# A graph attention layer on one core: the rows of every 32nd pair gathered as x in the node phase, and x_r computed in the rounds of edges

## The chip, the core and the metric

The kernel runs on one core of a Trainium2 chip. The core has a matrix engine (PE), three engines for elementwise work (VectorE or DVE, ScalarE or ACT, GpSimd or POOL), a sync engine (SP) that mostly issues DMAs, and 16 DMA engines. Each engine has a queue of its own and works through it in order; between engines there are semaphores only. The metric is the time on the device, in microseconds.

## The reference

12,500 nodes with 128 features, 400,000 edges sorted by their destination, 32 features an edge, 8 heads of 16.

```
h  = relu(layernorm(x))                       # 12500 x 128
ln = layernorm(h) * g1 + b1
x_l, x_r = ln @ W_l, ln @ W_r
m  = leaky_relu(x_l[src] + x_r[dst] + edge_attr @ W_e, 0.2)    # per edge; each node also has an edge to itself
alpha = per head: sum over 16 of m * att
a  = softmax of alpha over the edges of one destination
h2 = h + sum over edges of a * x_l[src] + bias
out = x + h2 + gelu(layernorm2(h2) @ W1 + b1) @ W2 + b2
```

What matters here: each edge needs the row `x_l[src]`, and `src` is random; `x_r[dst]` is needed in the order of the edges, since `dst` is sorted.

## The kernel before

Nodes are padded to 98 tiles of 128. The **node phase** (`tile_gnn`, lines 211 to 552) takes the tiles in 25 groups of four, `qs`, in a software pipeline: in round `r` the stages of `node_stages` (lines 514 to 527) work on group `r - late`. Statistics of x (`x_stats`, L421 to L423), relu of the normalised x in place in `h_sb` (L433), transposes (`h_turn`, L444), sums of squares (L458), the product with `[W_r | W_l]`, 256 columns (`product`, L468), scaling and bias on DVE (`x_lr`, L477). The result's x_l half, with eight columns of ones behind it (136 columns in all), goes to `xl_dram` (L485); the x_r half is split on POOL into three bf16 parts that add up to it (`split`, L492 to L496) and goes to `xs_dram`. The gain and the bias of the first norm are folded into the weights (`weights`). Between the rounds stand `from_first` (round 6: destinations as bf16 offsets from the first one of each unit; a cast on DVE, L336, and a subtraction on POOL, L340), `fits` (round 8: does the fast path apply?) and `edge_constants` (round 10). SP's queue has, in this order: x's first 16 tiles, the loads of `dst` (`load_dst`: `dc`, 111 rows of 14 KB, and `lu`, the last destination of each unit), the rest of x, constants (`load_consts`, with `att_c`, `we_sb` and `src_sb`), and then the stores of the phase.

The **rounds of edges** (`window_edges`) take 512 edges at a time, a *pair* of units of 256; there are 782 pairs. Everything is recorded by hand in order (`tc.manual_schedule`): in round `r` each entry `(late, f)` of `stages` does `f(r - late)`. For a pair `c`:

- `gather` in round c - 4: four indirect DMAs on POOL (L700), each 128 rows of 136 floats of `xl_dram`, by the column of `src_sb`. The buffers, `rows`, are a ring of twelve;
- `windows` in round c - 3, on SP: `ea` and `dlw` (the edges' features and destinations, for four pairs at a time, pool `load`) and `xrw`, the x_r parts of the 32 nodes the pair can touch;
- `place` (DVE, L728), one round ahead: which edge belongs to which node;
- `combine` in round c (PE): z = transposed rows (L742) + x_r of the destination (L745) + edge features (L746), one PSUM bank;
- `slope` (ACT, L752) and `bend` (DVE, L757) in c + 1: leaky relu; `score` (PE, L763, L764) in c + 2; `lowest` (DVE, L771) and `weigh` (ACT, exponential, L782) in c + 3; `turn` (PE, L790) in c + 4; `keep_turned` (ACT, L795) in c + 5; `collect` (PE, L804) in c + 6; `own_heads` (DVE, L813, L819) in c + 7; `put` (SP) in c + 8 writes the partial sums to `state`.

PSUM has eight banks: two each for `z`, `ab`, `pt_ps`, `acc`. Beside this, in the first 196 rounds the sum over all edge features is taken (`sum_load`, `sum_up`), and from round 199 on the 25 groups of nodes are finished by `steps` (`f_load` to `f_store`, 20 rounds a group, a new group every 23 rounds until they have caught up and every 32 then): the sums are put together, the feed-forward part is done and `out` is written. Their functions of ACT (root, gelu) need other tables than the exponential, which are loaded by ACT_TABLE_LOAD.

Of the kernel before, what the change touches and what calls it, by code (L numbers as in the profile page):

```python
# [46 lines left out]
SPARE = 8  # L47
BIG = 2.0**126
# [60 lines left out]
def heads_of(nc, pool, out, att_c):  # L109

    fh = pool.tile([P, H, C], F32, name="fh")
    iota(nc, fh, [[-1, H], [-H, C]], 0, 1)
    nc.vector.tensor_scalar(fh, fh, 0.0, None, op0=OP.is_equal)
    of = pool.tile([P, H], F32, name="of")
    nc.vector.tensor_reduce(of, fh, AX.X, OP.max)
    nc.vector.tensor_scalar(out, of, att_c, None, op0=OP.mult)
# [3 lines left out]
def tile_gnn(  # L120
# [46 lines left out]
    du_dram = dram.tile([RP * RU * U], BF16, name="du_dram")  # L167
    state = [dram.tile([NT * P * H, SH], F32, name=f"state{i}") for i in range(2)]
# [5 lines left out]
    flag = keep.tile([1, 1], I32, name="flag")  # L174

# [23 lines left out]
    lr_ps = pre.enter_context(tc.tile_pool(name="lr_ps", bufs=2, space=PSUM))  # L199
# [9 lines left out]
    quads = [(t, min(GN, NT - t)) for t in range(0, NT, GN)]  # L209
# [7 lines left out]
    def load_consts():  # L217
        for i, v in enumerate((ln2_g, ln2_b, None, b1[0:P], b1[P : 2 * P])):
            if v is not None:
                nc.sync.dma_start(cols[:, 2 + i : 3 + i], column(v))  # L220
        nc.sync.dma_start(att_c, bass.AP(tensor=att.tensor, offset=att.offset, ap=[[1, C], [C, H], [1, 1]]))
        nc.sync.dma_start(we_sb, bass.AP(tensor=w_e.tensor, offset=w_e.offset, ap=[[P, DE], [0, QP], [1, P]]))
        nc.sync.dma_start(w1_sb, w1)
        nc.sync.dma_start(w2_sb, w2.rearrange("(k p) f -> p k f", p=P))
        nc.sync.dma_start(bias_r, row_bcast(bias, P))
        nc.sync.dma_start(b2_r, row_bcast(b2, P))
        nc.sync.dma_start(src_sb, src)
        nc.sync.dma_start(first_sb, bass.AP(tensor=dst.tensor, offset=dst.offset, ap=[[0, 1], [U, NU]]))

# [40 lines left out]
    wlr = build.tile([P, 2, C, H], F32, name="wlr")  # L270
    bw_r = build.tile([P, 2, C, H], F32, name="bw_r")

    def weights():
        mean = build.tile([P, P], F32, name="mean")
        nc.vector.memset(mean, 1.0 / P)
        b_b = build.tile([P, P], F32, name="b_b")
        nc.scalar.copy(b_b, b1n_c.to_broadcast([P, P]))
        for i, w in enumerate((wr_sb, wl_sb)):
            nc.vector.tensor_scalar(wlr[:, i], w.rearrange("p (h c) -> p c h", c=C), g1_c, None, op0=OP.mult)
        wlr_f = wlr.rearrange("p s c h -> p (s c h)")  # L280
        ps = once_ps.tile([P, 2 * P], F32, name="w_ps")
        nc.tensor.matmul(ps, mean, wlr_f, start=True, stop=True)
        nc.vector.tensor_sub(wlr_f, wlr_f, ps)
        ps = once_ps.tile([P, 2 * P], F32, name="w_ps")
        for i, w in enumerate((wr_sb, wl_sb)):
            nc.tensor.matmul(ps[:, i * P : (i + 1) * P], b_b, w, start=True, stop=True)
        nc.vector.tensor_copy(bw_r, ps.rearrange("p (s h c) -> p s c h", s=2, h=H))

    def edge_constants():
# [4 lines left out]
        heads_of(nc, build, attbd, att_c)  # L294
# [3 lines left out]
        nh = build.tile([P, H, NW], F32, name="nh")  # L298
        iota(nc, nh, [[-1, H], [-H, NW]], 0, 1)
# [4 lines left out]
        own = build.tile([P, NW, H], F32, name="own")  # L304
        iota(nc, own, [[-1, NW], [0, H]], -NC3, 1)
        nc.vector.tensor_scalar(own, own, 0.0, None, op0=OP.is_equal)
        last = build.tile([P, NW, H], F32, name="last")
        iota(nc, last, [[0, NW], [0, H]], -NC3 - NW, 1)
# [3 lines left out]
        third = build.tile([P, CW], F32, name="third")  # L312
        iota(nc, third, [[-NS, CW]], 0, 1)
        group_range(nc, build, third, NS, CW)
        node = build.tile([P, CW], F32, name="node")
        iota(nc, node, [[1, CW]])
        nc.vector.tensor_mul(third, third, node)
        nc.vector.tensor_reduce(nid, third, AX.X, OP.add)
        unit = build.tile([P, 1], F32, name="unit")
        iota(nc, unit, [[0, 1]], -NC3, 1)  # L320
        nc.vector.tensor_scalar(unit, unit, 0.0, None, op0=OP.max)
        nc.vector.tensor_add(nid, nid, unit)
        fq = build.tile([P, QP, DE], F32, name="fq")
        iota(nc, fq, [[-1, QP], [-QP, DE]], 0, 1)
# [23 lines left out]
    def fits():  # L348
# [27 lines left out]
        place = rng.tile([RP, RU], F32, name="place")  # L376
        iota(nc, place, [[1, RU]], 0, RU)
# [17 lines left out]
    qs = [{"t0": t, "n": n, "h": h_sb[:, t : t + n, :]} for t, n in quads]  # L395

# [6 lines left out]
    def root_of(d, r, k):  # L403
        if r not in roots:
            roots[r] = (node.tile([P, 2, GN], F32, name="n_r", bufs=6), [0, 0])
        t, ns = roots[r]
        ns[k] = d["n"]
        d[f"r{k}"] = t[:, k, 0 : d["n"]]
        return d[f"r{k}"]

    def slots(r):
        if r not in roots:
            return []
        t, ns = roots[r]
        return [t] if ns == [GN, GN] else [t[:, k, 0:n] for k, n in enumerate(ns) if n]
# [14 lines left out]
    def relu(d, r):  # L430
        col(d, "sum")
        for t in range(d["n"]):
            nc.scalar.activation(  # L433
                d["h"][:, t, :], d["h"][:, t, :], AF.Relu,
                bias=d["m1"][:, t : t + 1], scale=d["r0"][:, t : t + 1], accum_out=d["sum"][:, t : t + 1],
            )

    def h_mean(d, r):
        nc.vector.tensor_scalar(d["sum"], d["sum"], -1.0 / P, None, op0=OP.mult)
# [14 lines left out]
    def h_square(d, r):  # L454
        col(d, "ssq")
        for t in range(d["n"]):
            sq = node.tile([P, P], F32, name="sq")
            nc.scalar.activation(  # L458
                sq, d["h"][:, t, :], AF.Square, bias=d["sum"][:, t : t + 1], accum_out=d["ssq"][:, t : t + 1]
# [4 lines left out]

    def product(d, r):
        d["lr"] = lr_ps.tile([P, GN, 2 * P], F32, name="lr")
        for t in range(d["n"]):
            nc.tensor.matmul(  # L468
                d["lr"][:, t, :], d["hT"][:, t, :], wlr.rearrange("p s c h -> p (s c h)"), start=True, stop=True
            )  # L470

    def x_lr(d, r):
        n = d["n"]
        d["xlr"] = node.tile([P, GN, P + XW], F32, name="xlr")
        nc.gpsimd.memset(d["xlr"][:, :, 2 * P :], 1.0)
        for t in range(n):
            nc.vector.scalar_tensor_tensor(  # L477
                d["xlr"][:, t, 0 : 2 * P],
                d["lr"][:, t, :],
                d["r1"][:, t : t + 1],  # L480
                bw_r.rearrange("p s c h -> p (s c h)"),
# [3 lines left out]
        nc.sync.dma_start(xl_t[:, d["t0"] : d["t0"] + n, :], d["xlr"][:, 0:n, P:])  # L485

    def split(d, r):
        n = d["n"]
        xr = d["xlr"][:, 0:n, 0:P]
        parts = node.tile([P, GN, NS, P], BF16, name="parts")[:, 0:n]  # L490
        left = node.tile([P, GN, P], F32, name="left")[:, 0:n]
        nc.gpsimd.tensor_copy(parts[:, :, 0, :], xr)  # L492
        nc.gpsimd.tensor_sub(left, xr, parts[:, :, 0, :])
        nc.gpsimd.tensor_copy(parts[:, :, 1, :], left)
        nc.gpsimd.tensor_sub(left, left, parts[:, :, 1, :])
        nc.gpsimd.tensor_copy(parts[:, :, 2, :], left)  # L496
        nc.sync.dma_start(xs_t[:, d["t0"] : d["t0"] + n, :, :], parts)
# [4 lines left out]
    def clear(g):  # L502
# [12 lines left out]
        (8, x_lr),  # L515
# [5 lines left out]
        (9, split),  # L521
    )
    LAST = 9
    with tc.manual_schedule():
        make_identity(nc, ident)
        load_weights()
        load_x(0, min(GN, NT))
        load_x(GN, min(3 * GN, NT - GN))
        load_dst()
        for t in range(4 * GN, NT, 14):  # L530
            load_x(t, min(14, NT - t))
        load_consts()
        nc.gpsimd.memset(empty, 0.0)
        nc.gpsimd.memset(empty[:, :, C + 1 : SH], CAP)
        for r in range(max(len(qs), 2) + LAST + 1):
            if r == 3:
                weights()
            if r == 6:
                from_first()
            if r == 8:  # L540
                fits()
            if r == 10:
                edge_constants()
# [4 lines left out]
            for late, f in node_stages:  # L548
                if 0 <= r - late < len(qs):
                    f(qs[r - late], r)  # L550
        clear(0)
# [3 lines left out]
    with tc.If(fast == 1) as cmp:  # L555
        window_edges(
            tc, n_edges, ea_t, NT, NE, NUE, ident, ident_b, wer, we_z, negrep, diag, nid, farw, bias_r, b2_r, w1_sb, w2_sb,
            cols, xl_dram, xl_t, xs_dram, xs_t, dc_dram, du_dram, state, clear, x_t, out_t, h_sb, src_sb, first_sb,
        )
    with cmp.Else():  # L560
        any_edges(
            tc, n_edges, dst, dst_tiles, ea_t, NT, NG, NCH, CPP, CP, ident, w_e, att, att_c, bias_r,
            xl_dram, xl_t, xs_t, h_sb, src_sb,
# [70 lines left out]
def window_edges(  # L634
    tc, n_edges, ea_t, NT, NE, NUE, ident, ident_b, wer, we_z, negrep, diag, nid, farw, bias_r, b2_r, w1_sb, w2_sb,
    cols, xl_dram, xl_t, xs_dram, xs_t, dc_dram, du_dram, state, clear, x_t, out_t, h_sb, src_sb, first_sb,
# [11 lines left out]
    AHEAD = 4  # L648
    WAHEAD = 3
# [6 lines left out]
    pairs = [{} for _ in range(n_pr)]  # L656

# [8 lines left out]
    with ExitStack() as es:  # L666
        once = es.enter_context(tc.tile_pool(name="e_once", bufs=1))
        load = es.enter_context(tc.tile_pool(name="e_load", bufs=3))
# [27 lines left out]
        def gather(c):  # L696
            xs = rows.tile([P, KP, XW], F32, name="xs")
            for t in tiles_of(c):
# [50 lines left out]
        def slope(c):  # L749
            d, e = pairs[c], sum(edges_of(c))  # L750
            d["zs"] = work.tile([P, EPR], F32, name="zs")
# [293 lines left out]
        def f_store(d):  # L1045
# [10 lines left out]
            (LATE + 1, own_heads),  # L1056
            (0, combine),
# [7 lines left out]
            (5, keep_turned),  # L1065
# [42 lines left out]
        def in_round(r, table):  # L1108
            for k, f in table:
                for d in groups:  # L1110
                    if d["round"] + k == r:
                        f(d)

        CLEAR = 8
        with tc.manual_schedule():
            for r in range(-AHEAD, max(last_round, groups[-1]["round"] + 20)):
# [11 lines left out]
                in_round(r, steps)  # L1128
                for late, f in late_stages:
# [5 lines left out]
def any_edges(  # L1135
    tc, n_edges, dst, dst_tiles, ea_t, NT, NG, NCH, CPP, CP, ident, w_e, att, att_c, bias_r,
    xl_dram, xl_t, xs_t, h_sb, src_sb,
# [31 lines left out]
    with tc.tile_pool(name="build", bufs=1) as build:  # L1169
        nc.vector.memset(attbd, 0.0)  # L1170
        for i in (0, LO):
            heads_of(nc, build, attbd[:, i : i + H], att_c)
# [6 lines left out]
        nc.vector.scalar_tensor_tensor(pick, kh, float(LO), high, op0=OP.is_equal, op1=OP.add)  # L1179

# [302 lines left out]
```

## Time and profile before

| | us |
|---|---|
| runs shown: median of 3 (lowest to highest) | 4172.99 (4167.11 to 4175.78) |
| the profiled execution: its time | 4170.51 |
| its span in the profile | 4168.6 |
| busy: PE / weight loads of PE | 3562.9 / 2472.1 |
| busy: DVE / ACT / POOL | 2433.0 / 1802.9 / 3073.7 |
| mean granted clock of PE | 0.946 |

A group in the profile is written "line engine operation output<-input"; a line of a timeline has the start and the length in us, the engine, the line and the operation, a count, and in brackets the idle time before it and what ended it. `PEld` is PE loading weights, `SPq` and `POOLq` are the queues in which DMAs are issued. "issue" names a wait that nothing in the profile explains. A line of the list of waits has the total, the count and the longest. PEclk is the granted clock of PE as a share of the full one.

### The profile page before, as it was taken

To read this page: it belongs to the slowest core of one execution; us is meant where nothing else is said; L and a number is where in the kernel's file an instruction comes from. 1 tells how busy PE (TensorE), PEld (TensorE's weight loads), DVE (VectorE), ACT (ScalarE), POOL (GpSimd) and SP (SyncE) were. 2 spreads that over 40 slices of the span, in tenths; PEclk is the share of its full clock that TensorE was granted. 3 is DMA by queue.
4 is the path that set the end of the run, shared out by engine and by line. 5 is a ranking of instruction groups with operands and counts; after the bars stand their busy time and mean duration, and the time that the engine had idled before them with its cause. 6 is when DMAs were issued, how large, how long until landed. Compare 5 with 4: busy or idle time off the path is not lost. (4 is left out here: it accounts for less than half of the span.)

```text
span 4168.6 us, 65325 instructions
## 1 busy us (share of the span) xinstructions
PE 3562.9 (85%) x18674; PEld 2472.1 (59%) x18675; DVE 2433.0 (58%) x5279; ACT 1802.9 (43%) x3939; POOL 3073.7 (74%) x3303
## 2 busy tenths in 40 slices
PE   2488888888888898989899989889889999988985
PEld 2355555655566666666666666566666666665654
DVE  6655656656665555655555555565556564655554
ACT  4533333333334444444444444444444444434433
POOL 3977777777777777777777777777777777777772
PEclk8799999999999999999999999999999999999998
DMA  5577777666656555555655566555566565555562
GB/s 150 172 169 182 182 180 179 156 153 159 150 118 116 115 116 119 115 112 115 125 117 117 117 119 120 117 117 105 117 122 118 117 120 113 107 117 104 114 123 51
DMA packets 631298, 535.20 MB, mean 128 GB/s; under 512 B 381763, under 2 KB 520882, under 8 KB 630690
## 3 DMA queue, kind: packets, MB, share of 16 engines
q1 hardware_dynamic: 530354, 313.00, 30.8%
q0 software_dynamic: 100000, 217.80, 29.6%
q8 instruction: 153, 2.51, 0.3%
q14 instruction: 215, 1.76, 0.2%
q10 hardware_dynamic: 576, 0.13, 0.0%
HBM read 477.18 MB, written 53.34 MB: 127 GB/s over the span
## 5 line engine op out<-in xcount | busy, mean ns | idle before, releaser
L700 POOL DMA_INDIRECT xs<-xl_dram,src_sb x3125 | 2955.1, 946 | 952.5 <-issue 808.9
L782 ACT ACTIVATE p<-ab,rec 128x256 f32<-128x256 f32 x1563 | 655.2, 470 | 1678.4 <-DVE rec L771 1654.1
L813 DVE TENSOR_TENSOR own<-acc,diag 128x272 f32<-128x272 f32 x782 | 344.7, 441 | 1360.3 <-PE acc L804 1353.6
L742 PE MATMUL z<-ident,xs 128*128 128x128 f32 x3125 | 585.7, 286 | 474.2 <-DMA xs<-xl_dram,src_sb 467.6
L742 PEld LDWEIGHTS z<-ident,xs 128*128 128x128 f32 x3125 | 405.0, 142 | 945.0 <-DMA xs<-xl_dram,src_sb 563.5
L804 PE MATMUL acc<-xs,pt 128*128 128x136 f32 x6250 | 884.6, 286 | 0.2 <-DVE f_yo L1051 0.2
L746 PE MATMUL z<-ea,we_z 128*128 128x512 f32 x1564 | 859.1, 633 | 0.0
L804 PEld LDWEIGHTS acc<-xs,pt 128*128 128x128 f32 x6250 | 812.5, 197 | 0.4 <-PE pt_ps L790 0.4
L764 PE MATMUL ab<-m,negrep 128*128 128x512 f32 x1564 | 801.1, 594 | 0.0
L752 ACT ACTIVATE zs<-z 128x512 f32<-128x512 f32 x782 | 474.7, 607 | 494.7 <-PE z L746 453.8
L790 PEld LDWEIGHTS pt_ps<-ident,p 128*128 128x128 f32 x3125 | 417.9, 149 | 453.6 <-issue 424.2
L771 DVE TENSOR_REDUCE rec<-ab 128x2 f32<-128x512 f32 x781 | 540.6, 692 | 135.9 <-PE ab L764 128.5
L757 DVE TENSOR_TENSOR m<-z,zs 128x512 f32<-128x512 f32 x782 | 532.2, 681 | 54.2 <-ACT zs L752 54.1
L790 PE MATMUL pt_ps<-ident,p 128*128 128x128 f32 x3125 | 498.2, 285 | 1.7 <-ACT pt L795 1.7
L795 ACT COPY pt<-pt_ps 128x512 f32<-128x512 f32 x782 | 457.6, 585 | 0.0
L819 DVE TENSOR_REDUCE rec<-own 128x34 f32<-128x272 f32 x782 | 341.0, 436 | 26.6
L746 PEld LDWEIGHTS z<-ea,we_z 128*128 128x128 f32 x1564 | 314.6, 201 | 35.7
L764 PEld LDWEIGHTS ab<-m,negrep 128*128 128x128 f32 x1564 | 301.8, 193 | 37.4 <-issue 0.7
L745 PE MATMUL z<-ne,xrw 128*128 128x512 bf16 x782 | 311.3, 398 | 0.0
L728 DVE TENSOR_SCALAR ne<-dlw,nid 112x512 bf16<-112x512 bf16 x782 | 288.5, 369 | 25.6 <-DMA dlw<-du_dram 25.6
L763 PE MATMUL ab<-ne,farw 128*128 128x512 bf16 x782 | 300.9, 385 | 0.0
L839 DVE TENSOR_REDUCE part<-ea_s 128x1 f32<-128x1024 f32 x98 | 118.5, 1209 | 0.0
(165 smaller groups left out, 1619.0 us busy)
## 6 DMA issues: line engine op xcount, KB each, us to landing
dlw<-dc_dram SPq DMA_DIRECT2D x196, 384.0 KB
ea<-in_ea_t SPq DMA_DIRECT2D x196, 256.0 KB
ea_s<-in_ea_t SPq DMA_DIRECT2D x98, 512.0 KB
xs<-xl_dram,src_sb POOLq DMA_INDIRECT x3125
state<-rec SPq DMA_DIRECT2D x1563, 9.0 KB
xrw<-xs_dram SPq DMA_DIRECT2D x782, 24.0 KB
state<-empty SPq DMA_DIRECT2D x28, 504.0 KB
st<-state SPq DMA_DIRECT2D x48, 288.0 KB
```

Source lines behind the costliest of these rows:

```text
L700: nc.gpsimd.indirect_dma_start(out=xs[:, j, :], out_offset=None, in_=xl_dram, in_offset=bass.IndirectOffsetOnAxis(ap=src_sb[:, c * KP + j ...
L742: nc.tensor.matmul(z[:, j * P : (j + 1) * P], d["xs"][:, j, 0:P], ident, start=(j == 0), stop=False, is_transpose=True)
L746: nc.tensor.matmul(z[:, :e], we_z[:, c % QP, :], d["ea"][:, :e], start=False, stop=True)
L752: nc.scalar.activation(d["zs"][:, :e], d["z"][:, :e], AF.Copy, scale=SLOPE)
L757: nc.vector.tensor_tensor(d["m"][:, :e], d["z"][:, :e], d["zs"][:, :e], op=OP.max)
L764: nc.tensor.matmul(ab[:, :e], negrep.rearrange("p n h -> p (n h)"), d["m"][:, :e], start=False, stop=True)
L771: nc.vector.tensor_reduce(d["rec"][:, :, CX], d["ab"].rearrange("p (u e) -> p u e", e=U), AX.X, OP.min)
L782: nc.scalar.activation(d["p"][:, us], d["ab"][:, us], AF.Exp, bias=d["rec"][:, i, CX:SH], scale=-1.0)
L790: nc.tensor.transpose(d["pt_ps"][:, js], d["p"][:, js], ident)
L795: nc.scalar.copy(d["pt"][:, :e], d["pt_ps"][:, :e])
L804: nc.tensor.matmul(d["acc"][:, i, :], d["pt"][:, j * P : (j + 1) * P], d["xs"][:, j, :], start=(j == js[0]), stop=(j == js[-1]),)
L813: nc.vector.tensor_tensor(own[:, :nu], d["acc"][:, :nu].rearrange("p u (c h) -> p u c h", h=H), diag[:, None].to_broadcast([P, nu, CX, H]) ...
```

## The change

Three things are moved.

1. **x_r.** The product of the node phase is with W_l alone (128 columns; `weights` folds the gain into W_l only), and `split` is gone. x_r is computed for each group of four tiles by `xr_steps`, eight steps of one round each: norm of `h_sb` (ACT), transposes (PE), gain and bias (ACT), the product with W_r (PE), three bf16 parts (ACT, DVE, ACT, DVE), the store. The first group does it in the rounds of the node phase; the others in the rounds of edges, from round 8 t0 - 18 on for the group that begins with tile t0: 14, 46, 78 and so on. Mean and root of each tile are kept for it in `mean_sb` and `roots_sb`.
2. **Every 32nd pair.** For the 24 pairs 40, 72, ... 776 the node phase gathers rows of x itself, not of x_l (`raw_gather`, four indirect DMAs of 128 rows of 512 bytes, on POOL, from a ring of five tiles), by indices loaded early on (`load_raw`), and stores them in `raw_dram`. In the rounds, `raw_steps` (twelve steps of one round each, starting nine rounds after those of x_r, at 23, 55, ...) loads them again and does what the node phase does: statistics, root, relu, transposes, squares, root, product with W_l, scaling and ones, store into `late_dram`. `gather` of such a pair is a plain DMA on SP from `late_dram`, two rounds after that store. The transposes and products of both kinds of steps use the PSUM ring `pt_ps`.
3. **Order and buffers.** `load_dst` comes after all of x; POOL's iotas come first (`count_up`); `edge_constants` is in round 7 (10 before), `from_first` in 12 (6), `fits` in 14 (8). `keep_turned` comes before `combine`, `slope` and `weigh` in a round and not after them, with the same pair. `load` has two buffers (three before), `zs` two (three), `lr_ps` three banks of half the size.

The diff, cut to this:

```diff
+def xr_round(t0, nt, n_edges):
+    first = (t0 * P - CW) * edges_per_node(nt, n_edges) // U - SPARE
+    return first // UP - WAHEAD - XR_STEPS - 1
+
+def raw_pairs(nt, n_edges):
+    n_pr = -(-n_edges // (UP * U))
+    at = [xr_round(t, nt, n_edges) + XR_STEPS + 1 for t in range(GN, nt, GN)]
+    return [(r + RAW_STEPS + AHEAD + 1, r) for r in at if r + RAW_STEPS + AHEAD + 2 < n_pr]
...
+    raw = [{"c": c, "i": i, "round": r, "n": UP * KU} for i, (c, r) in enumerate(raw_pairs(NT, n_edges))]
+    raw_dram = dram.tile([len(raw), P, UP * KU, P], F32, name="raw_dram")
+    late_dram = dram.tile([len(raw), P, UP * KU, XW], F32, name="late_dram")
...
+    def load_raw():
+        step = raw[1]["c"] - raw[0]["c"]
+        nc.sync.dma_start(
+            src_raw,
+            bass.AP(
+                tensor=src.tensor, offset=src.offset + raw[0]["c"] * UP * KU,
+                ap=[[NCH * K, P], [step * UP * KU, len(raw)], [1, UP * KU]],
+            ),
+        )
+
+    def raw_gather(d):
+        d["x"] = node.tile([P, UP * KU, P], F32, name="raw", bufs=5)
+        for j in range(d["n"]):
+            nc.gpsimd.indirect_dma_start(
+                out=d["x"][:, j, :],
+                out_offset=None,
+                in_=x,
+                in_offset=bass.IndirectOffsetOnAxis(ap=src_raw[:, d["i"], j : j + 1], axis=0),
+            )
+
+    def raw_store(d):
+        nc.sync.dma_start(raw_dram[d["i"], :, 0 : d["n"], :], d["x"][:, 0 : d["n"]])
...
     def product(d, r):
-        d["lr"] = lr_ps.tile([P, GN, 2 * P], F32, name="lr")
+        d["lr"] = lr_ps.tile([P, GN, P], F32, name="lr")
...
+    def xr_steps(pool, bank):
+        def norm(d):
+            off = pool.tile([P, GN], F32, name="xr_off")[:, 0 : d["n"]]
+            nc.vector.tensor_mul(off, d["mean"], d["r1"])
+            hn = tile_of(d, "hn", 0)
+            for t in range(d["n"]):
+                nc.scalar.activation(
+                    hn[:, t, :], d["h"][:, t, :], AF.Identity, bias=off[:, t : t + 1], scale=d["r1"][:, t : t + 1]
+                )
...
+        return norm, turn, turned, times, first, second, third, store
+
+    def raw_steps(pool, bank):
+        def load(d):
+            d["x"] = pool.tile([P, GN, P], F32, name="xr_0")[:, 0 : d["n"]]
+            nc.sync.dma_start(d["x"], raw_dram[d["i"], :, 0 : d["n"], :])
...
+        def store(d):
+            nc.sync.dma_start(late_dram[d["i"], :, 0 : d["n"], :], d["xl"])
+
+        return load, stats, root("r0"), scale, relu, turn, turned, var, root("r1"), times, rows, store
...
         load_weights()
         load_x(0, min(GN, NT))
+        load_raw()
         load_x(GN, min(3 * GN, NT - GN))
-        load_dst()
         for t in range(4 * GN, NT, 14):
             load_x(t, min(14, NT - t))
+        load_dst()
         load_consts()
...
-        for r in range(max(len(qs), 2) + LAST + 1):
+        rows_at = [i * 5 // 4 + (3 if i >= 10 else 0) for i in range(len(raw))]
+        for r in range(max(max(len(qs), 9) + LAST + 1, rows_at[-1] + 4)):
+            for d, at in zip(raw, rows_at):
+                if r == at:
+                    raw_gather(d)
+                if r == at + 3:
+                    raw_store(d)
             if r == 3:
                 weights()
-            if r == 6:
+            if r == 7:
+                edge_constants()
+            if r == 12:
                 from_first()
-            if r == 8:
+            if r == 14:
                 fits()
-            if r == 10:
-                edge_constants()
...
         def gather(c):
             xs = rows.tile([P, KP, XW], F32, name="xs")
+            if c in of_raw:
+                nc.sync.dma_start(xs, late_dram[of_raw[c]["i"]])
+                pairs[c]["xs"] = xs
+                return
...
             (LATE + 1, own_heads),
+            (5, keep_turned),
             (0, combine),
...
             (3, weigh),
-            (5, keep_turned),
             (-1, place),
...
                 in_round(r, steps)
+                in_round(r, enumerate(xr_steps), qs[1:])
+                in_round(r, enumerate(raw_steps), raw)
                 for late, f in late_stages:
```

## What I predicted, before the run

> **What bounds the kernel now.** I read the stretches of time first: the node phase up to the first gather, the gathers, and what comes after the last one.
>
> ```profile
> core 0: us, PE busy (x) PEld busy (x) DVE busy (x) ACT busy (x) POOL busy (x), PEclk, DMA share, GB/s
> 190.56:4097.97 3907.41, 3454.66 (x18196) 2390.78 (x18197) 2271.91 (x4722) 1685.36 (x3464) 2955.07 (x3125) 0.96 0.62 129
> 4097.97:4168.60 70.63, 32.43 (x179) 23.56 (x177) 25.67 (x61) 19.93 (x35) 0.00 (x0) 0.74 0.14 34
> 0.00:190.56 190.56, 75.83 (x302) 57.81 (x303) 135.45 (x496) 97.65 (x440) 118.61 (x179) 0.82 0.49 150
> ```
>
> By busy time PE (3455 of 3907 us) looks like the bound. The answer about line 700 and the list of waits say otherwise:
>
> ```profile
> L700 POOL DMA_INDIRECT xs<-xl_dram,src_sb x3125: 940/944/1223, 190.6 to 4097.0; - x196
> ```
>
> ```profile
> POOL xs L700 <- issue: 808.9, 2654, 0.3
> PE z L742 <- DMA xs<-xl_dram,src_sb: 467.6, 343, 27.9
> ```
>
> No wait of POOL before a gather is longer than 0.3 us, whatever is named as its end, and the gathers run from 190.6 to 4097.0 like a clock: 3906.5 us over 3124 intervals is **1.2505 us a gather** (0.944 of work and 0.30 between). PE, in contrast, waits for rows: 467.6 us, which is all of its idle time in that stretch (3907 - 3455 = 453, and a wait of 28 before it). So POOL's issue of gathers sets the time, 4 x 1.2505 = 5.00 us a round; PE needs 3455/782 = 4.42 us a round. The chain of waits on the page covers only the last 75 us and says nothing on this.
>
> The node phase ends like this on POOL:
>
> ```profile
> 188.71 0.40 POOL L496 CAST parts<-left 128x256 bf16<-128x256 f32 x1
> 189.45 0.93 POOL L683 MEMSET xrw<- 128x128 bf16 x6 [0.34 <-issue]
> 190.56 1.12 POOL L700 DMA_INDIRECT xs<-xl_dram,src_sb  x1 [0.17 <-issue]
> ```
>
> The split of x_r on POOL ends last: DVE's last `xlr` starts at 175.4. Earlier, DVE stood still for x, because SP was held by the issue of a load of `dst`:
>
> ```profile
> 7.64 22.74 SPq L258 DMA_DIRECT2D lu<-in_dst  x1
> 31.90 12.58 SPq L232 DMA_DIRECT2D h_sb<-in_x  x6
> 36.98 0.29 DVE L421 BATCH_NORM_STATS2 s<-h_sb 128x6 f32<-128x128 f32 x1 [18.94 <-DMA h_sb<-in_x]
> ```
>
> **The change, part by part.** The sum is against the profiled execution (4170.5 us, its span 4168.6); the median of the runs, 4173.0, is 2.5 us above it.
>
> *Gathers taken out of the rounds.* 24 pairs (40, 72, ... 776) are fetched by one plain transfer on SP; 24 x 4 = 96 gathers leave POOL's queue after the node phase and 3029 stay. If POOL stays the bound: 96 x 1.2505 = **-120 us** (3788 us of gathers). The DMAs wait in queues of their own, and a gather needs nothing that is new.
>
> *Does PE keep up?* Per block of 32 rounds the change adds on PE eight transposes and eight f32 products of 128 columns, which run as two passes: 8 x 0.161 (L997: 15.8 us for 98) + 16 x 0.123 (L1037: 48.3 for 392) = 3.3 us, in all 78. 3455 + 78 = 3533 of 3788, 93%. In a block that is 31 x 5.00 = 155.1 us of gathers against 144.6 of PE: 10.5 us to spare. A late pair gives POOL 5.0 us at once; PE makes up some 0.3 to 0.4 us a round, and twelve row buffers with four rounds of lead take such a lag without stopping POOL. Cost on the path: 0 within the stretch; if that cover went, the whole lag beyond 10.5 us a block would count. After the last late pair (776, six pairs from the end) PE has no time left to make it up: 0 to +10, I take **+4**.
>
> *ACT.* Per block: x_r 4 x 0.496 (L986) + 0.80 (L1001) + 2 x 0.56 = 3.9; late rows 4 x 0.48 (L433) + 4 x 0.39 (L458) + 2 x 0.2 = 3.9; and by the built program the table loads go from 100 to 194, four more a block at 1.283: 5.1. Together 12.9 x 24 = 310; 1685 + 310 = 1995 of 3788. *DVE.* x_r two passes of 0.69 and 0.17; late rows 4 x (0.267 + 0.182), a copy 0.68, four products of 128 columns at 0.20 to 0.47 (L279, L477), some seven small ones at 0.17: 6.5 a block, 156; 2272 + 156 = 2428. Both have over a third free. In the worst round ACT has its 2.0 us, a root with two table loads (2.8) and a step of the node groups (2.8): 7.6 us against 4.8, one round late. Behind it wait `p` and `pt`, needed by PE a round later; PE may slip by 3 us in such a round, inside the 10.5. Nothing counted.
>
> *keep_turned ahead in ACT's queue.* It now copies the transposes of the current round, and waits for PE's `turn` (2 us into a round); behind it stand `zs` and the next exponentials. ACT now idles 2.1 us a round waiting for DVE's `rec`, so 0; at worst 0.6 us later each round, off the path as `m` is used a round later. Two PSUM banks of `pt_ps` are now shared with the new steps: `turn` finds its bank free if ACT is under 4 us late. Fewer buffers (`load` 2, `zs` 2): ends 0 and 5 us at the start; 0.
>
> *SP and DMA.* Per block SP gets four more issues (0.4 to 0.5 us each), of which the store of x_r and the late store wait for DVE and ACT. What stands behind them are `xrw`, `ea`, `dlw` with three rounds of lead. 0.
>
> A rule that speaks against the added DVE work: the Trainium skill, page "SBUF — State Buffer", section "SBUF: two separate sides", says that a VectorE instruction in a two-port mode keeps GpSimd from writing descriptors, and that a gather of about 0.62 us then takes 3.1. By the page a dozen such hits a block would cost 24 x 12 x 2.5 = 720 us (an estimate). Here 3125 gathers beside 782 `ne` and all other DVE work never exceed 1.223 us, 0.28 over the median; the row decides, and I charge nothing.
>
> *The node phase.* POOL loses the split (25 x some 4.2 us) and gets 96 gathers of x (estimate 1.25 each, as L700, 120 us). DVE's product becomes 128 wide: 4 x 0.13 less a round. The order of SP's loads changes: x first, then `dst`, then the constants; `edge_constants` moves up from round 10 to 7 and needs constants that stand behind `dst`. Step by step: x (6.4 MB at some 345 GB/s, as it ran from 37 to 49 us, and a load of `src_raw` in 16-byte pieces between) is in by 26 us; `dc` takes as long as before (3 to 28 us, 25 us) to 51; `lu` and its successor 4 more; the constants up to `we_sb` 5 and 2 to land: **60 us**. DVE reaches round 7 at about 30 and waits there for 30 us, instead of 19 for x. From 60: constants 8.5; 17 rounds at 4.05 (now 4.43) 69; the cast and the subtraction on POOL, under which DVE stood still for 12.2, 14.4; `fits` 6.5; the last eight rounds 19 to 20: 179. The stores, POOL's barrier and its memsets: first gather at **185**. POOL's own line: 20 gathers of x to 37, then their stores wait behind the constants to 65, 20 more to 90, the subtraction to 102, 56 more to 172: not last. So **-5 us**; ends: -27 (DVE does not wait at round 7) and +25 (small pieces of `src_raw` hold up x by 10, rounds of 4.6 us, and gathers of x 10% slower).
>
> Sum: 4170.5 - 120 - 5 + 4 = 4049.5, say **4050 us**.
>
> **The rivals.**
> - *PE becomes the bound before POOL does.* Its work at full clock is 3533 x 0.96 = 3392 us; POOL's 3788 are passed at a mean granted clock under 0.895. For it: the busiest stretches show 0.93 to 0.95. Against: in this stretch the mean is 0.96. At 0.88 it is 3854, +66: 4116 us.
> - *The node phase gets longer.* For it: POOL's gathers of x wait for stores on SP, in a ring of five, and SP stands behind `dst`; the last late block could end last. Against: 13 us of room in the sum above. With 40 us more: 4090 us.
> - *The late fetch arrives late* (this one ends slower). It is issued on SP, in order, behind stores that wait for DVE; the longest such wait now is
>
> ```profile
> SPq L1052 <- DVE f_yo L1051: 313.6, 24, 31.5
> ```
>
>   If PE stood for S us at each late pair, 24 x (S - 10.5) would be lost; from S = 15.5 the gain is gone, at 20 it is 4050 + 228 = 4278 us. Against: the fetch goes out four rounds (19 us) ahead, `xrw` has only three behind the same waits, and PE's weight loads of `xrw` wait 0.3 us in all.
> - *The node phase gets much shorter*, as DVE and POOL lose work and x comes early: first gather at 155, 4020 us.
>
> **Chances.** The forecast 0.75 (4025 to 4075); PE the bound 0.08; a longer node phase 0.07; the late fetch late 0.05; a much shorter node phase 0.05. The range, 4020 to 4095, holds the forecast with its ends and most of the shorter and longer node phase, and leaves out some 0.16. Faster than 0.2% (about what a measurement of this kernel can tell from no change): all but the late fetch and a hundredth of PE's case, 0.94; same 0.01; slower 0.05.
>
> **What will show it.** Gathers on L896: 3029 of them, still 0.944 us and 1.25 apart, none waiting over 0.3 us; the first at about 185; PE's wait for `xs` down from 468 to some 250 us and its busy share near 93%; DVE with one wait of about 30 us for `we_sb` near 30 us. Wrong would be: gaps between gathers that end with PE (first rival), POOL's last gather of x after DVE's last `xl` (second), PE waits of over 10 us ending with `late_dram` (third).

## The result, and the profile after

The changed kernel takes 4054.92 us (median; 4053.53 to 4056.93) beside 4173.92 us for the kernel before: ratio 0.9718, 95% interval 0.9702 to 0.9733. The profiled execution took 4055.89 us, its span 4053.7. The forecast was 4050.

The stretches of time of the changed kernel, cut as before at the first edge gather and after the last one (columns: stretch, its length, busy time and instructions of each engine, TensorE clock, share of the DMA engines, GB/s):

```profile
core 0: us, PE busy (x) PEld busy (x) DVE busy (x) ACT busy (x) POOL busy (x), PEclk, DMA share, GB/s
0.00:186.38 186.38, 61.53 (x312) 52.98 (x313) 113.10 (x496) 99.48 (x447) 111.85 (x127) 0.69 0.58 172
186.38:3982.40 3796.02, 3460.77 (x18762) 2424.61 (x18763) 2400.80 (x5278) 2014.99 (x4155) 2872.94 (x3029) 0.97 0.66 139
3982.40:4053.70 71.30, 32.87 (x183) 23.89 (x181) 25.56 (x61) 20.69 (x36) 0.07 (x1) 0.74 0.14 34
```

The gathers' own line (least, median and greatest duration in ns, first and last start), and four rows of the list of waits (us in total, times, longest):

```profile
L896 POOL DMA_INDIRECT xs<-xl_dram,src_sb x3029: 940/945/1702, 186.4 to 3981.5; - x190
```

```profile
POOL xs L896 <- issue: 796.0, 2611, 0.3
...
PE z L938 <- DMA xs<-xl_dram,src_sb: 318.3, 317, 4.2
...
POOL raw L270 <- DMA raw_dram<-raw: 40.1, 1, 40.1
...
DVE wer L358 <- DMA we_sb<-in_w_e: 30.7, 1, 30.7
```

GpSimd still never waits over 0.3 us between edge gathers, so its issue still bounds the rounds. By starts, first gather, gathers and end were 190.6 + 3906.4 + 71.6 us before and are 186.4 + 3795.1 + 72.2 now: -4.2, -111.3, +0.6, together the 114.9 by which the spans differ. Two things are not as they were: the interval is 3795.1/3028 = 1.2533 us (1.2505 before), and the longest gather takes 1702 ns (1223).

The end of the node phase on GpSimd's timeline (start, duration, line, and in brackets the idle time before it with what ended it):

```profile
181.96 0.94 POOL L270 DMA_INDIRECT raw<-in_x,src_raw  x1 [0.30 <-issue]
185.29 0.94 POOL L875 MEMSET xrw<- 128x128 bf16 x6 [2.39 <-DMA raw<-in_x,src_raw]
186.38 0.95 POOL L896 DMA_INDIRECT xs<-xl_dram,src_sb  x1 [0.15 <-POOL xrw L875]
```

The gathers of raw rows run until 183 us and end the node phase; DVE's last `xl` starts at 169.9:

```profile
L527 DVE SCALAR_TENSOR_TENSOR xl<-lr,roots_sb,bl_r x98: 339/342/352, 67.5 to 169.9; 128x128 f32<-128x128 f32 x98
```

### The profile page after: what moved, and what is told of

The parts are those of the page before. It is cut to its first block, busy times and chain, and to the rows that moved or that the text cites. A ratio compares the mean times of both kernels' runs of the same rounds, so it can differ in the third digit from the quotient of the medians.

```text
span 4053.7 us, 65778 instructions
## 1 busy us (share of the span) xinstructions
PE 3555.2 (88%) x19254; PEld 2501.5 (62%) x19255; DVE 2539.5 (63%) x5834; ACT 2135.2 (53%) x4638; POOL 2984.9 (74%) x3156
## 4 chain that ended last, share of the span: by engine, by line
PE 40%; POOL 24%; DMA 22%; issue 13%; SPq 1%; DVE 0%; ACT 0%; POOLq 0%; DVEq 0%; ACTq 0%
POOL xs L896 22%; DMA xs<-xl_dram,src_sb 21%; PE z L942 9%; PE acc L1000 8%; PE ab L960 7%; PE pt_ps L986 4%; PE z L938 4%; PE z L941 2%; PE ab L959 2%; POOL raw L270 2%; PE acc L1233 1%; PE acc L1208 1%; DMA lu<-in_dst 1%; SPq L282 0%; DMA state<-rec 0%
## 5 line engine op out<-in xcount | busy, mean ns | idle before, releaser
L896 POOL DMA_INDIRECT xs<-xl_dram,src_sb x3029 | 2873.0, 949 | 923.2 <-issue 796.0
L938 PE MATMUL z<-ident,xs 128*128 128x128 f32 x3125 | 573.3, 283 | 353.0 <-DMA xs<-xl_dram,src_sb 318.3
L1000 PE MATMUL acc<-xs,pt 128*128 128x136 f32 x6250 | 874.9, 284 | 0.2 <-DVE f_yo L1247 0.2
L942 PE MATMUL z<-ea,we_z 128*128 128x512 f32 x1564 | 835.4, 617 | 0.0
L1000 PEld LDWEIGHTS acc<-xs,pt 128*128 128x128 f32 x6250 | 802.6, 195 | 0.4 <-PE pt_ps L986 0.4
L986 PEld LDWEIGHTS pt_ps<-ident,p 128*128 128x128 f32 x3125 | 407.8, 146 | 438.2 <-issue 386.4
L986 PE MATMUL pt_ps<-ident,p 128*128 128x128 f32 x3125 | 489.2, 281 | 2.2 <-ACT pt L991 1.3
L270 POOL DMA_INDIRECT raw<-in_x,src_raw x96 | 95.5, 995 | 71.3 <-DMA raw_dram<-raw 40.1
```

What stands on the lines that cost most here:

```text
L896: nc.gpsimd.indirect_dma_start(out=xs[:, j, :], out_offset=None, in_=xl_dram, in_offset=bass.IndirectOffsetOnAxis(ap=src_sb[:, c * KP + j ...
L938: nc.tensor.matmul(z[:, j * P : (j + 1) * P], d["xs"][:, j, 0:P], ident, start=(j == 0), stop=False, is_transpose=True)
L942: nc.tensor.matmul(z[:, :e], we_z[:, c % QP, :], d["ea"][:, :e], start=False, stop=True)
L986: nc.tensor.transpose(d["pt_ps"][:, js], d["p"][:, js], ident)
L1000: nc.tensor.matmul(d["acc"][:, i, :], d["pt"][:, j * P : (j + 1) * P], d["xs"][:, j, :], start=(j == js[0]), stop=(j == js[-1]),)
```

## Theories

**A.** GpSimd's queue is the bound from end to end: a gather costs its 1.25 us wherever it stands. The change gains what GpSimd spent before the first edge gather on splitting x_r and on waiting, which the 96 gathers now fill. **B.** The node phase has a length of its own; each gather taken out of the rounds gains its whole 1.25 us. **C.** TensorE paces the rounds. **D** (formed on the trace of after): the long gathers are held by VectorE's new subtraction for x_r's third part (L586), which reads both operands from SBUF.

## Experiments

**e1: no late pairs** (x_r still in the rounds).

```diff
-        load_raw()
...
-            for d, at in zip(raw, rows_at):
-                if r == at:
-                    raw_gather(d)
-                if r == at + 3:
-                    raw_store(d)
...
-    of_raw = {d["c"]: d for d in raw}
+    raw = []
+    of_raw = {}
```

> The change without its late pairs: x_r stays in the rounds, all 3125 gathers stay on GpSimd's queue in the rounds, none runs in the node phase. Theory A (a gather costs GpSimd its 1.2533 us wherever it runs; the change gains what GpSimd had idled or split before the first edge gather): without the 96 gathers of raw rows the node phase ends earlier, with VectorE (113 us busy and 31 us of waiting for we_sb), first edge gather at 155 us (145 to 170); 155 + 3125 x 1.2533 + 71 = 4143 us (4130 to 4160). Theory B (the node phase is as long anyway, each gather taken out of the rounds is worth its whole 1.2533 us): 186 + 3917 + 71 = 4174 us. Theory C (TensorE sets the pace of the rounds, not the gathers): 4055 us or less, since TensorE has less to do.

4147.13 us, ratio to before 0.9945 (0.993 to 0.9961). The gathers' line, and the two long waits of GpSimd:

```profile
L890 POOL DMA_INDIRECT xs<-xl_dram,src_sb x3125: 940/944/1607, 165.5 to 4077.1; - x196
```

```profile
POOL xrw L869 <- DMA xl_dram<-xl: 74.5, 1, 74.5
...
POOL dlb L393 <- DVE df L389: 73.8, 1, 73.8
```

A, within 4 us; B is 27 us off, C 92. Without raw rows GpSimd idles 148 us of the node phase, which now ends with the last store of x_l, at 165.5 us and not the 155 expected. The late pairs are thereby told apart from the rest of the change. Moving x_r, with the new order and buffers: 25.1 us off the node phase, 5.2 more on the gathers (3911.6 us for the same 3125), 3.3 off the end, 23 gained in all. The late pairs, from e1 to the changed kernel: 116.5 off the gathers, 20.9 more in the node phase, 3.9 at the end, 92 gained in all.

**e2: every second late pair (first diff); e3: two late pairs in 32 (second diff).**

```diff
-    return [(r + RAW_STEPS + AHEAD + 1, r) for r in at if ...]
+    return [(r + RAW_STEPS + AHEAD + 1, r) for r in at[::2] if ...]
```

```diff
-    at = [xr_round(t, nt, n_edges) + XR_STEPS + 1 for t in ...]
+    at = [xr_round(t, nt, n_edges) + XR_STEPS + i * RAW_STEPS for t in ... for i in range(2)]
```

In e3 `load_raw` also fetches the indices with two loads.

> Late pairs at every 64th pair only: 48 gathers in the node phase, 3077 in the rounds. Theory A: GpSimd does its first 20 gathers, waits for the store until 71 us and needs 28 x 1.25 + 12 us from there, which ends before VectorE's 155 us; so first edge gather at 155 us, 155 + 3077 x 1.2533 + 71 = 4083 us (4070 to 4100). Theory B: 186 + 3856 + 71 = 4114 us, half way to the kernel without late pairs. Theory C: 4055 us or less.

> Two late pairs in every 32: some 190 gathers in the node phase, some 2933 in the rounds. Theory A: the node phase grows by what the rounds lose, first edge gather at 307 us, 307 + 2933 x 1.2533 + 71 = 4054 us (4045 to 4075), no gain over the changed kernel. Theory B: 186 + 3676 + 71 = 3934 us. Theory C (TensorE, then some 3525 us busy of 3676, becomes the bound): 4080 to 4110 us, with gathers that wait for it over 0.3 us.

e2: 4091.32 us, 0.9812 (0.9797 to 0.9827). e3: 4050.34, 0.9714 (0.9699 to 0.9729). The edge gathers of e2, then the raw gathers and the edge gathers' stretch of e3:

```profile
L896 POOL DMA_INDIRECT xs<-xl_dram,src_sb x3077: 940/944/1626, 171.3 to 4019.3; - x193
```

```profile
L272 POOL DMA_INDIRECT raw<-in_x,src_raw x188: 940/944/4473, 7.0 to 299.8; - x188
```

```profile
303.80:3983.50 3679.70, 3434.43 (x19034) 2438.65 (x19035) 2484.62 (x5738) 2207.65 (x4659) 2784.82 (x2937) 0.98 0.65 147
```

First gather at 165.5, 171.3, 186.4 and 303.8 us for 0, 48, 96 and 188 raw gathers (155 and 307 were expected for 48 and 188). The first 48 lengthen the node phase by 6 us: they fill GpSimd's idle time. The last 92 lengthen it by 117.4, 1.28 us each, and save 3795.1 - 3678.8 = 116.3 in the rounds: nothing is left. B's 3934 us is out. C is out too: with 188 gathers moved, TensorE is busy 93% of the stretch and no gather waits over 0.3 us. By a line of 1.28 us a gather back from 186.4 to the 171 of e2, GpSimd becomes last in the node phase at about 84 raw gathers (worked out, not run).

**e4: x_r's remainder in PSUM** (`xr` is the bank that holds the product). The steps `second` and `third` become empty, so that the whole split stands in one round.

```diff
-            nc.vector.tensor_sub(tile_of(d, "left", 0), xr, d["parts"][:, :, 0, :])
+            nc.vector.tensor_sub(xr, xr, d["parts"][:, :, 0, :])
+            nc.scalar.copy(d["parts"][:, :, 1, :], xr)
+            nc.vector.tensor_sub(d["parts"][:, :, 2, :], xr, d["parts"][:, :, 1, :])
```

The reason for it, in the changed kernel's timeline (DVE and GpSimd, other engines left out):

```profile
2936.84 0.34 DVE L924 TENSOR_SCALAR ne<-dlw,nid 112x512 bf16<-112x512 bf16 x1
2936.90 1.70 POOL L896 DMA_INDIRECT xs<-xl_dram,src_sb  x1 [0.31 <-issue]
...
2937.10 0.68 DVE L586 TENSOR_TENSOR xr_parts<-xr,xr_parts 128x512 bf16<-128x512 f32 x1
...
2938.91 0.94 POOL L896 DMA_INDIRECT xs<-xl_dram,src_sb  x1 [0.30 <-issue]
```

Of the 14 gathers over 1.15 us, 12 lie beside an L586; eight of these, without a `ne` before it, take 1.21 to 1.30, the four right after a `ne` 1.44 to 1.70. All 12 end 0.81 to 0.82 us after that L586 does. The other 12 L586 of the rounds have no gather over 1.12 us beside them.

> The remainder of x_r's split is kept in PSUM, so that VectorE's last subtraction has one operand in PSUM and one in SBUF in place of two in SBUF; the three steps of the split stand in one round. Theory D (the gathers of 1.2 to 1.7 us are held by this subtraction, some 24 times by 0.2 to 0.75 us): the longest gathers go, their mean falls from 949 to 947 ns, the time by 5 us to 4050 us (4047 to 4053). Rival (they are long for another reason, as transfers beside them): 4055 us, the mean still 949 ns and the same gathers long.

4044.76 us, 0.9704 (0.9691 to 0.9717). Its gathers:

```profile
L898 POOL DMA_INDIRECT xs<-xl_dram,src_sb x3029: 940/944/1234, 186.6 to 3973.7; - x190
```

The long gathers are gone; the interval is 3787.1/3028 = 1.2507 us, as in the kernel before. The new round of the subtraction isn't the reason: its 24 runs start from 0.68 us before a gather to 0.94 us after its start, and every gather beside them takes 0.940 to 0.947 us. The one of 1.234 stands beside other work of VectorE. D holds, but for less than the 10 us between the medians (5 were expected). For each trace I took what the gathers over 0.97 us have beyond 0.945 (lengths to a hundredth of a us), and the stretch of the 3029 gathers less that:

| kernel | stretch, first to last gather | beyond 0.945 us | the rest |
|---|---|---|---|
| after | 3795.1 | 10.3 | 3784.8 |
| e9, e11, e12 (with L586 as it is) | 3792.2, 3790.1, 3791.2 | 11.3, 8.9, 10.3 | 3780.9, 3781.2, 3780.9 |
| e4, e10 (one operand in PSUM) | 3787.1, 3788.2 | 5.9, 7.1 | 3781.2, 3781.1 |
| before, its 3124 intervals scaled to 3028 | 3786.4 | 5.3 | 3781.1 |

D is worth some 4 us. Another 4 are in the execution of the changed kernel that was profiled: its gathers of up to 0.97 us take 945.1 ns on average, those of the kernel before, e1, e4 and e9 to e12 943.7 to 943.8, and 3029 times the difference is 3.9 us. The kernel before, too, took 3.4 us more beside it (4173.92) than beside e4 (4170.47). The changed kernel itself was not run again. The rest of the 10 is in the end, which is 3.5 us shorter in e4's profile.

**e5 to e8, and again as e9 to e12.** When e5 to e8 first ran, every engine's queue stood still between instructions, so that the kernel before took 4931.97 us; only differences among the four can be read there. The same kernels then ran beside a kernel before of 4170.65 us, and those times are used.

The shorter node phase (e5, e9): stores of raw rows on ACT's queue, constants ahead of `dst`, the subtraction (and `fits`) four rounds later, and the raw gathers' pause of three rounds after 13 late pairs in place of 10.

```diff
-        nc.sync.dma_start(raw_dram[...], d["x"]...)
+        nc.scalar.dma_start(raw_dram[...], d["x"]...)
...
+        load_consts()
         load_dst()
-        load_consts()
...
-            if r == 12:
+            if r == 16:
                 from_first()
...
```

> The changed kernel with a shorter node phase: the stores of the raw rows issued on ScalarE's queue in place of SyncE's, the small constants loaded ahead of the loads of dst, dlb four rounds later. Theory A (GpSimd's gathers of raw rows end the node phase, and 40 us of its 186 us are a wait for the first store, which stands behind the loads of dst): GpSimd runs nearly without a wait, 8 + 96 x 1.25 + 12 us, first edge gather at 145 to 152 us; the rest as in the changed kernel: 4055 - 37 = 4018 us (4010 to 4025). Rival (VectorE or ScalarE, not GpSimd, set the length of the node phase): VectorE loses at most its 31 us of waiting but runs beside the gathers, first edge gather at 165 to 175 us, 4033 to 4045 us.

> The kernel of e5 once more, since in that call every engine's queue stood still between instructions (the kernel before took 4932 us there, the gathers 1.50 us each) and the stretches can't be set against those of the changed kernel. Where the kernel before takes 4170 us again: Theory A: first edge gather at 145 to 152 us, 4018 us (4010 to 4025). Rival (VectorE and ScalarE pace the node phase once GpSimd doesn't wait for the first store): first edge gather at 160 to 175 us, 4028 to 4045 us.

e5: 4840.52 us; e9: 4042.46, 0.9695 (0.9679 to 0.9711). First gather at 177.8, not 145 to 152: GpSimd's expected node phase fell. The time is in the rival's bracket; the first gather is later than even the rival's 160 to 175. The waits of e9, and what SP issued:

```profile
DVE xl L527 <- DMA xl_dram<-xl: 23.8, 3, 22.1
...
POOL dlb L393 <- DVE df L389: 21.3, 1, 21.3
...
POOL raw L270 <- DMA raw_dram<-raw: 8.5, 5, 2.7
```

```profile
54.38 21.52 SPq L308 DMA_DIRECT2D lu<-in_dst  x1
77.44 0.23 SPq L314 DMA_DIRECT2D lu<-in_dst  x1
77.77 20.08 SPq L535 DMA_DIRECT2D xl_dram<-xl  x8
```

GpSimd's wait for the stores fell from 40.1 us to 8.5, and a new one of 21.3 took its place. The load of `dst` (L308) holds SP's queue at either place, for 21.5 us here and 25.6 in the changed kernel. Now the stores of x_l are behind it: DVE waits for a free x_l buffer, and GpSimd's subtraction for DVE. So A holds for the rounds; how long the node phase is hangs on SP's loads and on VectorE as well. Loads of `dst` that hold no queue were not tried.

Both together (e6, e10): the diffs of e5 and e4.

> The kernel with the shorter node phase and the remainder of x_r's split in PSUM, both. Theories A and D together: the two gains lie in different stretches of the same queue and add up: 4018 - 9 = 4009 us (4000 to 4017). If either were covered by the other: 4018 or 4045 us.

> The kernel of e6 once more. Theories A and D together: 10 us less than e9, as e4 was 10 us less than the changed kernel: 4008 us (4000 to 4017). If the one gain covered the other: no difference from e9.

e6: 4838.78 us; e10: 4040.16, 0.9687 (0.9671 to 0.9703), 2.3 us under e9 where 10 were expected. The stretch of the gathers is 4.0 us shorter than e9's, as D has it; in the profiled runs the end took 5 us more. By the ratios e10 is the fastest of all, 0.3% under the changed kernel, with intervals that just touch (0.9703 and 0.9702).

The added work for the late pairs twice (e7, e11); the second result is not stored:

```diff
+        again_steps = raw_steps[:-1]
+        again = [{**d, "round": d["round"] + RAW_STEPS} for d in raw]
...
+                in_round(r, enumerate(again_steps), again)
```

> The changed kernel with the eleven steps that turn raw rows into x_l run a second time for each late pair, twelve rounds later, their result not stored: the work that the change adds for the late pairs doubled on TensorE, VectorE and ScalarE, no gather and no store more. Theory A (that work lies beside the gathers, which alone set the pace): 4055 us, at most 3 us more. Theory C (the rounds pay for it): TensorE's some 40 us, or the 12 us or so of ScalarE in each of 24 blocks on its way to TensorE, 4075 to 4150 us.

> The kernel of e7 once more (the added work for the late pairs done twice, the second result not stored). Theory A: 4055 us, at most 5 us more. Theory C: 4075 to 4150 us.

e7: 4863.97 us; e11: 4050.94, 0.9717 (0.97 to 0.9733). The stretch of e11's gathers:

```profile
187.90:3979.00 3791.10, 3469.55 (x18826) 2449.51 (x19040) 2488.63 (x5752) 2215.29 (x4676) 2867.88 (x3029) 0.97 0.63 141
```

ACT is busy 200 us more than in the changed kernel, DVE 88, and it costs nothing: C and every price for the arithmetic of the late pairs are out.

keep_turned at its old place (e8, e12):

```diff
-            (5, keep_turned),
             (0, combine),
...
             (3, weigh),
+            (5, keep_turned),
```

> The changed kernel with the copy of the turned weights (keep_turned) back at its old place at the end of ScalarE's list. Theory A (no engine but GpSimd is late, the place is worth nothing): 4055 us (4051 to 4059). Rival (its new place gives TensorE its operand earlier and is part of the gain): the table loads and added steps of ScalarE come ahead of it, TensorE's lag grows and the end after the last gather with it: 4062 to 4080 us.

> The kernel of e8 once more (keep_turned at its old place). Theory A: 4055 us (4051 to 4059). Rival: 4062 to 4080 us.

e8: 4867.83 us; e12: 4049.9, 0.9712 (0.9696 to 0.9729): its place is worth nothing, as A says (1 us under A's range). Of the first runs, e8 and e7 lie 4 us apart in 4864. The smaller buffers were not varied alone.

## Why the prediction was right, step by step

The time was right, and so was the bound; one step was right by two errors that cancel.

- *The bound.* As told: 3029 gathers, none waiting over 0.3 us. e3 and e11 put it to the test from both sides.
- *Term 1, -120 us:* -111.3. The 96 gathers are worth the 120 (3028 x 1.2505 = 3786.5); the interval did not stay at 1.2505. Of the 8.6 us lost, 5.0 lie in the gathers over 0.97 us, most of it L586's, as e4 shows; the other 3.6 are that execution's (the table at e4).
- *The rule I charged nothing for.* I quoted the rule on two-port modes from the Trainium skill, page "SBUF — State Buffer", section "SBUF: two separate sides"; its 3.1 us are for a DMA that GpSimd issues, not for a gather in particular. L586 falls under another rule of that section, which I did not weigh: a VectorE instruction with two inputs in SBUF contends with a GpSimd instruction that reads SBUF. I took the greatest gather of a trace in which L586 did not exist, 1.223 us, for a bound on the new work. Between the 720 us (my estimate from the page) and my 0, the runs show about 5: without L586's two operands in SBUF the long gathers have 5.9 and 7.1 us beyond 0.945 (e4, e10), close to the 5.3 of before, so that VectorE's other new work adds little, and the one subtraction, 24 times, nearly all.
- *TensorE keeps up.* Estimate 78 us more, 93% busy, waits for `xs` of 250; measured 91% and 318. The seven costliest groups of matmuls, the same number of them, took 63 us less than before (the second operand of `z` 617 ns for 633), so that busy time rose by 6: the added work is some 69 us by that account (an estimate, as the groups overlap on TensorE). ACT 2015 (1995 forecast), DVE 2401 (2428). Nothing was on the path.
- *Term 3, +4 us at the end:* +0.6. Over the profiles of this study the end is 68 to 75 us long, so neither can be told from 0.
- *Term 2, -5 us in the node phase:* -4.2, by another cause than given. DVE's wait for `we_sb` was as told (30.7 us, to 57). But DVE's last `xl` came at 169.9, not 179; and GpSimd's raw gathers, which I had end at 172 ("not last"), ended at 183 and set the start. I had their second run start at 65 us; it started at 71.5, and two gathers took 2.5 and 3.8 us, beside VectorE's cast for `from_first` (L389, 2.27 us) and its reduction in `fits` (L404, 3.88 us); each ended 0.8 us after that instruction. So the sign that I had named for the second rival, a last gather of x after DVE's last `xl`, came, at no cost against the forecast, because DVE was 10 us earlier too; that the two errors cancel is luck. e1 shows it: without the raw gathers the start is at 165.5.
- *The late fetch* never shows: no wait of TensorE ends with a transfer of `late_dram`.
- *What the working missed as a whole.* I priced the raw gathers (120 us) and the gathers saved (120 us) in two places and did not set one against the other. On one queue they are the same 1.25 us. The gain is the 102 us of splitting (28.4 + 28.4 + 15.2 + 15.2 + 15.0) and some of the waiting that left GpSimd's node phase (its gaps of over 0.4 us add up to 63.5 us before and 45.2 after). That is why a second set of late pairs, which the working would have priced at -116, is worth nothing.

## What to carry to other kernels

Where one queue is the bound, work moved along that queue gains only up to the idle time at the place to which it is moved: write down the queue's busy and idle time in both stretches before you price the move, and find the point at which the idle time is used up. Work taken from that queue and given to engines with a third to spare makes room of its whole time, but the room is worth that only when other work of the queue fills it: the 102 us of splitting gained 23 alone (e1) and 115 with the raw gathers in their place. And the new engine's operands matter: an instruction with both in SBUF can still hold the queue it was meant to free.

## What the runs showed of the hardware that was not expected

- A VectorE subtraction of 128x512 with both operands in SBUF lengthened 12 of the gathers beside it (there were 24 such subtractions) from 0.94 us: eight to between 1.21 and 1.30, and four, where it follows a bf16 `ne` of 0.34 us at once, to between 1.44 and 1.70. In the seven profiles that have L586 as it is and ran at 1.25 us a gather (the changed kernel, e1 to e3, e9, e11, e12), all 78 gathers of over 1.15 us beside one end 0.81 to 0.82 us after it. With one operand in PSUM no gather beside it takes over 0.947 us; the longest of all are 1.234 (e4) and 1.274 (e10), beside other work of VectorE. The section named above says that such an instruction contends with a GpSimd one that reads SBUF; the gathers, which read their indices there, agree. It works the other way too: in the changed kernel's node phase the same subtraction, 0.68 us otherwise, starts beside GpSimd's two subtractions for `dlb` (100.55 to 112.83 us) and ends 0.56 us after them:

```profile
101.42 11.97 DVE L586 TENSOR_TENSOR xr_parts<-xr,xr_parts 128x512 bf16<-128x512 f32 x1
```

- When e5 to e8 first ran, the gathers kept their 0.944 us, but GpSimd stood still for some 2.2 us, in most cases after every eighth one (e5 has 403 gaps of over 1 us between gathers, 337 of them eight gathers after the last), and other engines had such gaps too; the interval was 1.503 us (e5). Here is e8:

```profile
2008.01 0.94 POOL L896 DMA_INDIRECT xs<-xl_dram,src_sb  x1 [0.30 <-issue]
2011.20 0.94 POOL L896 DMA_INDIRECT xs<-xl_dram,src_sb  x1 [2.25 <-remote]
```

  What held the queues there was not found. These four, and the kernel before beside them, ran on another chip (number 2) than e1 to e4 and e9 to e12 (number 11); whether it was the chip or the moment no run tells.
